# A hybrid convolution-attention kernel on one core: where four branch weights and sixteen filter scales are computed

## The chip, the cores and the metric

The kernel runs on one core of a Trainium2 chip. The metric is the device time of one execution in microseconds. All arithmetic is float32.

## The reference, cut to what matters

The input is `x` of shape (2, 128, 64, 64). Layer 0 normalises it by groups and runs a 7 x 7 neighbourhood attention with its projections and layer norms, then a small feed-forward part. Layer 1 turns the image into 2 x 4096 tokens of 128 channels, adds a self-attention whose queries, keys and values are the same normalised tokens (the diagonal is masked), and then the ffn: a sum over four branches of spectral filters and short lags.

```python
for i, frac in enumerate((1, 2, 4, 8)):
    xi = x[:, :T // frac]
    si = _stu(xi, sigma, phi, M_u[i], M_phi_plus[i], M_phi_minus[i])
    outs.append(jnp.pad(si, ((0, 0), (0, T - si.shape[1]), (0, 0))))
y_soft = softmax((log_weights + gumbel) / TEMPERATURE)
y_hard = one_hot(argmax(y_soft), 4)
weights = y_hard - stop_gradient(y_soft) + y_soft
return jnp.sum(jnp.stack(outs, axis=-1) * weights, axis=-1)
# inside _stu: s = sigma ** 0.25 scales the 16 filters' matrices
```

The weights depend only on `log_weights` and `gumbel`, four numbers each, and the scales only on `sigma`, sixteen numbers.

## The kernel before, in words

The 128 channels or 128 tokens lie on the partitions. **Layer 0** goes through 16 bands (8 per image) of 8 image rows. Each band is cut into named pieces (`p.*` the projections, `u0.*` to `u3.*` the four units of attention, `r.*` and `t.*` what follows it, `k.*` the first tokens of layer 1), and a table `PLAN` gives each piece a due time; a band starts every `PERIOD` = 2300 of the plan's units, so several bands are in flight. All pieces become `events`, sorted by due time, and those in the list `now` are issued inside `tc.manual_schedule` for TensorE (PE), VectorE (DVE), ScalarE (ACT) and GpSimd (POOL): the order on those four queues is the order of the list. SP, which issues the loads and stores (the band's values to memory at L479, its windows back at L496), is not in that set. What is left over of the last bands goes into the list `later`.

**Layer 1** begins with `attention(0, fill)`. It runs over 36 pairs of 512-token chunks; `weights` makes a tile of scores (L905), masks the diagonal (L911, VectorE) and takes the exponential (L913, ScalarE); `turned` transposes tiles (L929) and takes them out with VectorE (L932); L943 and L970 multiply by the tokens. After every other step `fill()` takes one step from the generators in `steps`: first `drain()`, which issues `later` by threes, then `chosen` (the function `branch_weights`), then `filters()`, then `tokens(1, bank)`. `branch_weights` loads `log_w`, `gumbel` and `sigma`, computes `sg = sigma ** 0.25` on GpSimd, the softmax and the one-hot masks in some 23 tiny VectorE instructions, the weights `wt`, the masks `seg` by segment, and at last `mixed(mu, m_u)`, the weighted sum of the branches' short-lag matrices. `attention(1, fill)` does the second image; its steps include `for_ffn`, which opens tiles in the space of the first image's tokens and mixes the ffn's matrices in `filter_matrices` (L1146, L1148, then scaled by `sg` at L1163 and L1164). Then comes the ffn itself, L1379 and L1391, some 900 us of matmuls.

Outside `tc.manual_schedule` the order of each engine's queue is drawn by the compiler from a priority in program order and from what is ready.

Of the kernel before, what the change touches and what calls it, by code (L numbers as in the profile page):

```python
# [8 lines left out]
F32 = mybir.dt.float32  # L9
# [5 lines left out]
P = 128  # L15
# [6 lines left out]
KF = 16  # L22
# [73 lines left out]
def kernel(  # L96
# [62 lines left out]
    mhalf = const.tile([P, KF], F32, name="mhalf")  # L159
    nc.vector.memset(mhalf, -0.5)  # L160
    seg = const.tile([P, NBR], F32, name="seg")


    def rsqrt(dst, var, eps):
# [61 lines left out]
    with l0a:  # L226
# [523 lines left out]
        def behind():  # L750
# [22 lines left out]
            nc.vector.tensor_copy(wg[:, W_2:W_3], pb[:, 0:P])  # L773
            yield

        events = []
        for k, (b, g) in enumerate(order):
            t = {}
# [23 lines left out]
        gn1 = group_norm(1)  # L802
        for i in range(7):
            events.append((2 * PERIOD + i * PERIOD // 3 + 50, None, "", lambda: next(gn1)))
        events.sort(key=lambda e: e[0])


# [52 lines left out]
    with ap_:  # L860
# [11 lines left out]
        tr = tp.tile([P, 2, NC], F32, name="tr")  # L872
        nc.sync.dma_start(out=tr, in_=nc.inline_tensor(t_in, "t_in").ap().rearrange("(h p) c -> p h c", p=P))
        sg = tp.tile([P, KF], F32, name="sg")
        wt = tp.tile([P, NBR], F32, name="wt")
        one = tp.tile([P, 512], F32, name="one")
        nc.gpsimd.memset(one, 1.0)

# [212 lines left out]
                        )  # L1091
                    yield

        def branch_weights():

            lw = sp.tile([P, NBR], F32, tag="lw", name="lw")
            gu = sp.tile([P, NBR], F32, tag="gu", name="gu")
            nc.sync.dma_start(out=lw, in_=log_w.partition_broadcast(P))
            nc.sync.dma_start(out=gu, in_=gumbel.partition_broadcast(P))
            nc.sync.dma_start(out=sg, in_=sigma.partition_broadcast(P))  # L1100
            yield
            quarter = sp.tile([P, KF], F32, tag="quarter", name="quarter")
            nc.gpsimd.memset(quarter, 0.25)
            nc.gpsimd.tensor_tensor(sg, sg, quarter, ALU.pow)

            z = sp.tile([P, NBR], F32, tag="z", name="z")
            nc.vector.tensor_tensor(z, lw, gu, ALU.add)
            m = sp.tile([P, 1], F32, tag="zm", name="zm")
            nc.vector.tensor_reduce(m, z, AX.X, ALU.max)
            nc.vector.tensor_scalar(z, z, m, None, ALU.subtract)  # L1110
            ys = sp.tile([P, NBR], F32, tag="ys", name="ys")
            tot = sp.tile([P, 1], F32, tag="tot", name="tot")
            nc.scalar.activation(ys, z, AF.Exp, bias=0.0, scale=1.0, accum_out=tot)
            nc.vector.reciprocal(tot, tot)
            nc.vector.tensor_scalar(ys, ys, tot, None, ALU.mult)
            yield
            nc.vector.tensor_reduce(m, ys, AX.X, ALU.max)

            oh = sp.tile([P, NBR], F32, tag="oh", name="oh")
            nc.vector.tensor_scalar(oh, ys, m, None, ALU.is_equal)  # L1120
            seen = sp.tile([P, NBR], F32, tag="seen", name="seen")
            nc.vector.tensor_copy(seen[:, 0:1], oh[:, 0:1])
            for i in range(1, NBR):
                nc.vector.tensor_tensor(seen[:, i : i + 1], seen[:, i - 1 : i], oh[:, i : i + 1], ALU.max)
            for i in range(NBR - 1, 0, -1):
                nc.vector.tensor_tensor(oh[:, i : i + 1], seen[:, i : i + 1], seen[:, i - 1 : i], ALU.subtract)
            yield

            for j in range(NBR):
                nc.vector.tensor_copy(seg[:, j : j + 1], seen[:, NBR - 1 - j : NBR - j])  # L1130
            nc.vector.tensor_tensor(wt, oh, ys, ALU.subtract)
            nc.vector.tensor_tensor(wt, wt, ys, ALU.add)

            yield
            mixed(mu, m_u)
            yield

        def mixed(dst, src):
            dst2 = dst.rearrange("p k e -> p (k e)")
            for i in range(NBR):  # L1140
                st = sp.tile([P, 4, P], F32, tag="st", name="st")
                n = src.shape[1]
                nc.sync.dma_start(out=st[:, 0:n], in_=src[i].rearrange("k d e -> d k e"))
                st2 = st[:, 0:n].rearrange("p k e -> p (k e)")
                if i == 0:
                    nc.vector.tensor_scalar(dst2, st2, wt[:, 0:1], None, ALU.mult)  # L1146
                else:
                    nc.vector.scalar_tensor_tensor(dst2, st2, wt[:, i : i + 1], dst2, ALU.mult, ALU.add)  # L1148
# [18 lines left out]
        def filters():  # L1167

            fr = sp.tile([P, 2, 4 * BINS], F32, tag="fr", name="fr", bufs=1)
            nc.sync.dma_start(out=fr, in_=nc.inline_tensor(t_filter, "t_filter").ap().rearrange("(a p) c -> p a c", p=P))  # L1170

            def lags(c0):

                pn = sp.tile([P, KF, 2, LG], F32, tag="st", name="pn")
                nc.sync.dma_start(
                    out=pn.rearrange("p k l f -> p (k l) f"),
                    in_=bass.AP(phi_pad.tensor, P - FB + c0 * FB, [[FB, P], [PHW, 2 * KF], [1, LG]]),
                )
# [12 lines left out]

            def more(m, j):
                banks[m] = bank()
                rows_ = slice(j % 2 * SB, (j % 2 + 1) * SB)
                nc.tensor.matmul(
                    banks[m], lhsT=fr[rows_, j // 2, m * P : (m + 1) * P],
                    rhs=ph[j // 2][rows_].rearrange("p l f k -> p (l f k)"), start=True, stop=True,
                )

            def keep(m, j):  # L1200
                if j == 0:
                    sums[m] = sp.tile([P, 512], F32, tag="sum", name="sum", bufs=2)
                    nc.scalar.copy(sums[m], banks[m])
                else:
                    nc.vector.tensor_tensor(sums[m], banks[m], sums[m], ALU.add)
                nb = P // 4
                nc.sync.dma_start(
                    out=gs[m * nb : (m + 1) * nb, :, SG - 1 - j].rearrange("g r (o c) -> (g r) o c", o=2), in_=sums[m]
                )

            begin = [4 * (m // 2) + m % 2 for m in range(4 * BINS // P)]
            for slot in range(begin[-1] + SG):
                mine = [(m, slot - s0) for m, s0 in enumerate(begin) if 0 <= slot - s0 < SG]
                for mj in mine:
                    more(*mj)
                for mj in mine:
                    keep(*mj)
                yield
# [35 lines left out]
        def drain():  # L1254

            rings[:] = [(ps_m, "bank")] * 2
            for i, f in enumerate(later):
                f()
                if i % 3 == 2:
                    yield  # L1260
            l0.close()
            tp1 = ap_.enter_context(tc.tile_pool(name="l1_t1", bufs=1, side="right"))
            tt[1] = tp1.tile([P, NT, P], F32, name="tt1")
            tok[1] = tp1.tile([P, NT, P], F32, name="tok1")
            cm[1] = tp1.tile([P, T], F32, name="cm1")
            yield

        chosen = branch_weights()
        next(chosen)
        steps = [drain(), chosen, filters(), tokens(1, bank)]  # L1270
        fill, left = filler(0, steps)
        attention(0, fill)
        for gen in steps:
# [28 lines left out]
        def for_ffn():  # L1302

            nonlocal mpl, mmi, inv, mu1, ctp
            while spare != [None]:
                yield True
            first_.close()
            l1 = ctx.enter_context(tc.tile_pool(name="l1", bufs=1))
            mpl = l1.tile([P, KF, P], F32, name="mpl")
            mmi = l1.tile([P, KF, P], F32, name="mmi")  # L1310
            mu1 = l1.tile([P, 3, P], F32, name="mu1")
            inv = l1.tile([P, 3, CB], F32, name="inv")
            ctp = ctx.enter_context(tc.tile_pool(name="blocks", bufs=5))
            nc.gpsimd.tensor_copy(mu1, mu)
            yield from filter_matrices(mpl, mmi)

            nc.sync.dma_start(out=inv, in_=nc.inline_tensor(t_out, "t_out").ap().rearrange("(a p) c -> p a c", p=P))
            for s, (lo, hi) in enumerate(((0, 32), (32, 64), (64, 128), (128, 256))):
                nc.vector.tensor_scalar(inv[:, :, lo:hi], inv[:, :, lo:hi], seg[:, s : s + 1], None, ALU.mult)
            yield  # L1320
            yield from load_blocks()
# [251 lines left out]
```

## Time and profile before

| what | us |
|---|---|
| median of 3 runs | 2194.35 |
| lowest, highest | 2192.41, 2196.59 |
| profiled execution, its own time | 2194.31 |
| its span | 2192.6 |
| TensorE busy | 2141.4 |
| VectorE busy | 952.3 |
| ScalarE busy | 769.8 |
| GpSimd busy | 278.5 |
| L1104, the power of `sg`, GpSimd | 3.17, at 351.48 |
| L1107 to L1132, weights and masks, VectorE | from 342.10 to 348.35 |
| L1143 and on, the ffn's matrices mixed | 945 to 1020 |

The span is the time from the first to the last instruction; the execution's own time has 1.7 us around it. Layer 0 ends at about 340 to 345, the first attention at about 800, the second at about 1290. Durations in the trace are those of single instructions on the engine; those of TensorE are modelled at their ends. Two consecutive instructions of one engine can overlap by a few hundredths of a microsecond.

### The profile page before, as it was taken

What the parts mean: (1) busy time and instruction counts of PE and PEld (TensorE: products, weight loads), DVE (VectorE), ACT (ScalarE), POOL (GpSimd) and SP (SyncE); (2) the same over time, 40 slices, a digit from 0 to 9 for tenths busy, and PEclk for the clock granted to TensorE, in tenths of its full rate; (3) what the DMA queues carried; (4) which work ended last, traced back from release to release, by engine and by line L of the source; (5) the groups of instructions that cost most, each with busy time, mean ns of one, the idle gap of its engine ahead of it and who ended that gap; (6) DMA issues with size and microseconds to landing.
All of it is one profiled execution on the core that took longest, in us unless ns stands there. A gap on an engine that the chain in (4) does not pass through costs nothing.

```text
span 2192.6 us, 32071 instructions
## 1 busy us (share of the span) xinstructions
PE 2141.4 (98%) x12016; PEld 1339.1 (61%) x12016; DVE 952.3 (43%) x3150; ACT 769.8 (35%) x1904; POOL 278.5 (13%) x359
## 2 busy tenths in 40 slices
PE   6899998999999999999999999999999999999998
PEld 4677765545555444544555456776767676767776
DVE  5899986444443353366333543222232323232232
ACT  3889883222332222222223233222232323232232
POOL 3477874200000000000000000000000000000000
PEclk8999999999999999999999999999999999999999
DMA  4222212011000011043000142121221212212101
GB/s 147 62 62 61 62 53 53 0 68 53 25 24 25 19 34 44 1 138 87 1 24 25 49 112 55 45 60 43 57 54 46 52 48 46 54 46 55 40 11 77
DMA packets 170347, 110.56 MB, mean 50 GB/s; under 512 B 21311, under 2 KB 155087, under 8 KB 169680
## 3 DMA queue, kind: packets, MB, share of 16 engines
q1 hardware_dynamic: 169266, 105.01, 17.7%
q8 instruction: 95, 1.56, 0.3%
q0 software_dynamic: 576, 2.10, 0.3%
q10 hardware_dynamic: 350, 1.41, 0.3%
q14 instruction: 60, 0.49, 0.1%
HBM read 73.86 MB, written 34.63 MB: 49 GB/s over the span
## 4 chain that ended last, share of the span: by engine, by line
PE 87%; DVE 5%; POOL 3%; DMA 2%; ACT 1%; issue 1%; SPq 0%; POOLq 0%; DVEq 0%; ACTq 0%
PE acc L1391 26%; PE pc L1379 13%; PE own L943 10%; PE bank L905 9%; PE other L970 8%; PE bank L929 4%; PE bank L335 2%; PE bank L1082 2%; PE bank L545 2%; PE bank L195 2%; PE bank L1034 1%; PE py L1413 1%; DMA st<-in_m_minus_dram 1%; PE bank L509 1%; PE po L567 1%
## 5 line engine op out<-in xcount | busy, mean ns | idle before, releaser
L1380 DVE COPY y<-pc 128x512 f32<-128x512 f32 x320 | 221.3, 692 | 350.8 <-PE pc L1379 347.2
L913 ACT ACTIVATE e<-bank 128x512 f32<-128x512 f32 (+3 forms) x288 | 161.6, 561 | 511.6 <-PE bank L905 384.7
L1391 PE MATMUL acc<-y,mpl 128*128 128x256 f32 x1280 | 292.2, 382 | 0.0
L1391 PE MATMUL acc<-y,mmi 128*128 128x256 f32 x1280 | 288.1, 379 | 0.0
L1379 PE MATMUL pc<-ct,ut 64*128 64x512 f32 x1280 | 285.5, 596 | 0.0
L905 PE MATMUL bank<-cm 128*128 128x512 f32 (+3 forms) x576 | 277.6, 564 | 1.4 <-DVE y L656 1.4
L1391 PEld LDWEIGHTS acc<-y,mpl 128*128 128x128 f32 x1280 | 238.3, 190 | 59.2 <-issue 29.6
L1391 PEld LDWEIGHTS acc<-y,mmi 128*128 128x128 f32 x1280 | 242.8, 190 | 32.4
L1380 ACT COPY y<-pc 128x512 f32<-128x512 f32 x320 | 204.8, 640 | 91.8 <-PE pc L1379 91.7
L943 PE MATMUL own<-et,tok 128*128 128x512 f32 x448 | 227.8, 595 | 4.4 <-DVE part L932 4.3
L970 PE MATMUL other<-e,tok 128*128 128x512 f32 x448 | 229.0, 593 | 0.0
L1379 PEld LDWEIGHTS pc<-ct,ut 64*128 64x128 f32 x1280 | 120.6, 187 | 145.9 <-issue 140.2
L932 DVE CUSTOM_DVE_ANT_0 et<-bank,one 128x512 f32<-128x512 f32 x224 | 145.9, 686 | 121.5 <-PE bank L929 121.2
L1398 ACT COPY ob<-acc 128x256 f32<-128x256 f32 x32 | 19.3, 604 | 387.1 <-PE acc L1391 387.1
L943 PEld LDWEIGHTS own<-et,tok 128*128 128x128 f32 x448 | 83.9, 190 | 113.8 <-issue 65.1
L1415 DVE TENSOR_TENSOR xa<-py,xa 128x512 f32<-128x512 f32 x32 | 22.1, 692 | 281.4 <-PE py L1413 281.4
L970 PEld LDWEIGHTS other<-e,tok 128*128 128x128 f32 x448 | 81.9, 190 | 89.7 <-issue 87.2
L929 PEld LDWEIGHTS bank<-ident,e 128*128 128x128 f32 x896 | 102.9, 141 | 54.3 <-issue 49.3
L905 PEld LDWEIGHTS bank<-cm 128*128 128x128 f32 x576 | 93.9, 191 | 64.1 <-issue 43.5
L167 POOL TENSOR_TENSOR ln_rs<-ln_rs,mhalf 128x4 f32<-128x4 f32 x24 | 24.2, 1007 | 775.4 <-DVE ln_rs L166 775.4
L532 ACT ACTIVATE p<-p,mn 128x196 f32<-128x196 f32 x256 | 114.3, 449 | 14.2 <-DVE mn L522 13.6
L929 PE MATMUL bank<-ident,e 128*128 128x128 f32 x896 | 117.3, 274 | 0.0
(227 smaller groups left out, 2339.8 us busy)
## 6 DMA issues: line engine op xcount, KB each, us to landing
ut<-us SPq DMA_DIRECT2D x80, 256.0 KB
us<-ub SPq DMA_DIRECT2D x64, 256.0 KB
vw<-vd SPq DMA_DIRECT2D x256, 49.0 KB
ct<-gs SPq DMA_DIRECT2D x160, 72.0 KB
ct<-gs SPq DMA_DIRECT2D x160, 64.0 KB
gs<-sum SPq DMA_DIRECT2D x20, 256.0 KB
vd<-v SPq DMA_DIRECT2D x128, 32.0 KB
st<-in_m_plus_dram SPq DMA_DIRECT2D x16, 256.0 KB
```

The costliest lines, as they stand in the source:

```text
L195: nc.tensor.transpose(ps[:, j * P : (j + 1) * P], src[:, j, :], ident)
L335: nc.tensor.matmul(pl, lhsT=wg[:, lo : lo + P], rhs=zT, start=True, stop=True)
L532: nc.scalar.activation(p, p, AF.Exp, bias=t[name + "mn"][:, h : h + 1], scale=-1.0, accum_out=t["den"][:, u, h : h + 1],)
L905: nc.tensor.matmul(ps[:, lo:], lhsT=cm[b][:, n * P : (n + 1) * P], rhs=cm[b][:, CHUNKS[c] * 512 + lo : (CHUNKS[c] + 1) * 512], start=True, ...
L913: nc.scalar.activation(e[:, lo:], ps[:, lo:], AF.Exp, bias=0.0, scale=ASCALE, accum_out=part[:, n, c : c + 1])
L929: nc.tensor.transpose(pt[:, k * P : (k + 1) * P], es[k][:, m * P : (m + 1) * P], ident)
L932: nc.vector.tensor_tensor_reduce(et, pt, one, 1.0, 0.0, ALU.mult, ALU.add, part[:, n, a : a + 1])
L943: nc.tensor.matmul(own, lhsT=tok[b][:, n, :], rhs=e, start=first, stop=last)
L970: nc.tensor.matmul(other, lhsT=tok[b][:, 4 * CHUNKS[a] + j, :], rhs=es[j], start=(j == 0), stop=(j == 3))
L1379: nc.tensor.matmul(pc, lhsT=ut[fp, b, par, :], rhs=cv_[fp], start=True, stop=True)
L1380: (nc.scalar.copy if f else nc.vector.tensor_copy)(y[:, 4 * f : 4 * f + 4, :, par, b * 2 * FB + q : (b + 1) * 2 * FB : 2], pc.rearrange("p ...
L1391: nc.tensor.matmul(acc, lhsT=(mmi if l else mpl)[:, k, :], rhs=y[:, 1::2, k, ::-1, :] if l else y[:, 0::2, k, :, :], start=(l == 0 and k = ...
```

## The change

`branch_weights` moves into layer 0 as four events of the hand-written order, at due times `(len(order) - 4) * PERIOD + 450 * i + 100`, that is in band 12 of 16: its two loads, the softmax, the masks, then `seg` and `wt`. Its tiles move from the layer-1 pool to the `const` pool. `sigma` is no longer loaded there: its load, the memset of 0.25 and the power stand in `for_ffn`, ahead of `filter_matrices`. In layer 1 the four steps of `chosen` become one step, `own_lags`, which holds only `mixed(mu, m_u)`.

```diff
+    wt = const.tile([P, NBR], F32, name="wt")
...
+        def branch_weights():
+            lw = const.tile([P, NBR], F32, name="lw")
+            gu = const.tile([P, NBR], F32, name="gu")
+            nc.sync.dma_start(out=lw, in_=log_w.partition_broadcast(P))
+            nc.sync.dma_start(out=gu, in_=gumbel.partition_broadcast(P))
+            yield
+            z = const.tile([P, NBR], F32, name="lw_gu")
+            nc.vector.tensor_tensor(z, lw, gu, ALU.add)
...
+            nc.scalar.activation(ys, z, AF.Exp, bias=0.0, scale=1.0, accum_out=tot)
+            nc.vector.reciprocal(tot, tot)
+            nc.vector.tensor_scalar(ys, ys, tot, None, ALU.mult)
+            yield
+            nc.vector.tensor_reduce(m, ys, AX.X, ALU.max)
+            oh = const.tile([P, NBR], F32, name="oh")
+            nc.vector.tensor_scalar(oh, ys, m, None, ALU.is_equal)
...
+            yield
+            for j in range(NBR):
+                nc.vector.tensor_copy(seg[:, j : j + 1], seen[:, NBR - 1 - j : NBR - j])
+            nc.vector.tensor_tensor(wt, oh, ys, ALU.subtract)
+            nc.vector.tensor_tensor(wt, wt, ys, ALU.add)
+            yield
...
+        weights_ = branch_weights()
+        for i in range(4):
+            events.append(((len(order) - 4) * PERIOD + 450 * i + 100, None, "", lambda: next(weights_)))
         events.sort(key=lambda e: e[0])
...
-        def branch_weights():
-            lw = sp.tile([P, NBR], F32, tag="lw", name="lw")
...
-            nc.sync.dma_start(out=sg, in_=sigma.partition_broadcast(P))
-            yield
-            quarter = sp.tile([P, KF], F32, tag="quarter", name="quarter")
-            nc.gpsimd.memset(quarter, 0.25)
-            nc.gpsimd.tensor_tensor(sg, sg, quarter, ALU.pow)
...
-            yield
-            mixed(mu, m_u)
-            yield
...
-        chosen = branch_weights()
-        next(chosen)
-        steps = [drain(), chosen, filters(), tokens(1, bank)]
+        def own_lags():
+            mixed(mu, m_u)
+            yield
+
+        steps = [drain(), own_lags(), filters(), tokens(1, bank)]
...
             nc.gpsimd.tensor_copy(mu1, mu)
+            nc.sync.dma_start(out=sg, in_=sigma.partition_broadcast(P))
+            quarter = sp.tile([P, KF], F32, tag="quarter", name="quarter", bufs=1)
+            nc.gpsimd.memset(quarter, 0.25)
+            nc.gpsimd.tensor_tensor(sg, sg, quarter, ALU.pow)
             yield from filter_matrices(mpl, mmi)
```

More of the change, by code (lines that the diff above doesn't have):

```diff
@@ L774, in behind @@
             yield
+        def branch_weights():
[6 more added lines that the diff above has]
+            nc.vector.tensor_tensor(z, lw, gu, ALU.add)
+            m = const.tile([P, 1], F32, name="zm")
+            nc.vector.tensor_reduce(m, z, AX.X, ALU.max)
+            nc.vector.tensor_scalar(z, z, m, None, ALU.subtract)
+            ys = const.tile([P, NBR], F32, name="ys")
+            tot = const.tile([P, 1], F32, name="tot")
+            nc.scalar.activation(ys, z, AF.Exp, bias=0.0, scale=1.0, accum_out=tot)
[5 more added lines that the diff above has]
+            nc.vector.tensor_scalar(oh, ys, m, None, ALU.is_equal)
+            seen = const.tile([P, NBR], F32, name="seen")
+            nc.vector.tensor_copy(seen[:, 0:1], oh[:, 0:1])
+            for i in range(1, NBR):
+                nc.vector.tensor_tensor(seen[:, i : i + 1], seen[:, i - 1 : i], oh[:, i : i + 1], ALU.max)
+            for i in range(NBR - 1, 0, -1):
+                nc.vector.tensor_tensor(oh[:, i : i + 1], seen[:, i : i + 1], seen[:, i - 1 : i], ALU.subtract)
+            yield
[4 more added lines that the diff above has]
+            yield
         events = []
@@ L874 @@
         sg = tp.tile([P, KF], F32, name="sg")
-        wt = tp.tile([P, NBR], F32, name="wt")
         one = tp.tile([P, 512], F32, name="one")
@@ L1092, in short_lags @@
                     yield
-        def branch_weights():
-            lw = sp.tile([P, NBR], F32, tag="lw", name="lw")
-            gu = sp.tile([P, NBR], F32, tag="gu", name="gu")
-            nc.sync.dma_start(out=lw, in_=log_w.partition_broadcast(P))
-            nc.sync.dma_start(out=gu, in_=gumbel.partition_broadcast(P))
-            nc.sync.dma_start(out=sg, in_=sigma.partition_broadcast(P))
-            yield
-            quarter = sp.tile([P, KF], F32, tag="quarter", name="quarter")
-            nc.gpsimd.memset(quarter, 0.25)
[L1104 to L1115, printed above, removed]
-            yield
[L1117 to L1126, printed above, removed]
-            yield
[L1129 to L1134, printed above, removed]
-            mixed(mu, m_u)
-            yield
         def mixed(dst, src):
```

## The prediction

> **What bounds the kernel now.** I read the page's first line of totals, then stretches by engine, then the chain of waits and the timeline around the two places that the edit touches.
>
> ```profile
> PE 2141.4 (98%) x12016; PEld 1339.1 (61%) x12016; DVE 952.3 (43%) x3150; ACT 769.8 (35%) x1904; POOL 278.5 (13%) x359
> ```
>
> TensorE fills 98% of 2192.6 us, so a change that adds no matmul can only win back the 51 us in which it is not busy, or make more of them. The stretches (us; busy time of each engine and, in brackets, instructions; then granted clock, DMA share, GB/s) say where they lie:
>
> ```profile
> 219.00:274.00 55.00, 54.77 (x812) 40.86 (x811) 51.77 (x275) 49.31 (x153) 48.65 (x62) 1.00 0.23 62
> 301.00:320.00 19.00, 17.35 (x273) 12.59 (x272) 15.60 (x84) 14.94 (x48) 13.47 (x18) 1.00 0.22 63
> 320.00:340.00 20.00, 16.94 (x239) 12.03 (x237) 12.45 (x63) 12.09 (x38) 11.51 (x16) 0.83 0.22 64
> 340.00:366.00 26.00, 22.21 (x119) 12.28 (x118) 18.25 (x80) 8.62 (x26) 21.09 (x23) 1.00 0.39 70
> 366.00:900.00 534.00, 529.59 (x1893) 265.96 (x1894) 220.44 (x751) 149.29 (x401) 31.54 (x36) 1.00 0.10 30
> ```
>
> The reader is to see three regimes. In layer 0's steady bands (219 to 274) four engines are close to full: VectorE 94%, ScalarE 90%, GpSimd 88%, and the chain of work passes from one to the next, so there a microsecond on VectorE is not free. From 301 to 366, the end of layer 0 and the start of layer 1, TensorE idles 1.65 + 3.06 + 3.79 = 8.5 us. From 366 to 900 it lacks 4.4 us in 534: nothing placed there shows.
>
> **What the Trainium skill says.** "TensorE: Matmul & The Clock Gate", Part 1, says that the clock falls to half after an idle window of some 3.4 us and that the window runs freely. The trace agrees: the clock is 0.50 from about 332.9 to 339.7, 6.8 us, hence the 0.83 above. "VectorE: DVE Perf Modes", The DRAIN you can't avoid, says that each VectorE instruction pays a flush before the next starts. The trace's 128x4 operations, each fed by the one before, start 0.18 to 0.20 us apart for a few elements. "Perfetto Trace Analysis", Tensor Engine Instruction, says that VectorE, ScalarE and GpSimd run strictly in order; the waits below agree.
>
> **Part 1: the weights leave the start of layer 1.** The timeline today (start, duration, engine, line; in brackets the idle time before it):
>
> ```profile
> 342.10 0.15 DVE L1107 TENSOR_TENSOR z<-lw,gu 128x4 f32<-128x4 f32 x1
> 343.27 0.23 DVE L1115 TENSOR_SCALAR ys<-ys,tot 128x4 f32<-128x4 f32 x1
> 345.78 0.80 DVE L1120 TENSOR_SCALAR oh<-ys,zm 128x4 f32<-128x4 f32 x1
> 347.80 0.29 DVE L911 TENSOR_TENSOR bank<-bank,ndiag 128x128 f32<-128x128 f32 x1
> 348.25 0.60 ACT L913 ACTIVATE e<-bank 128x512 f32<-128x512 f32 x1 [5.21 <-DVE wt L1131]
> 351.48 3.17 POOL L1104 TENSOR_TENSOR sg<-sg,quarter 128x16 f32<-128x16 f32 x1
> 354.22 0.36 DVE L695 BATCH_NORM_AGGREGATE kmv<-ln_st 128x2 f32<-128x6 f32 x4
> 354.67 0.23 POOL L700 TENSOR_SCALAR krs<-kmv 128x4 f32<-128x4 f32 x1
> ```
>
> The first softmax tile of layer 1 waits for L911, and L911 stands behind the masks. VectorE ends `y` at 345.86 and the first matmul of L905 (346.01, four in 1.74 us, so 0.43 each) is done by about 346.5. Without L1120 to L1130 L911 could start at 346.55, that is 1.25 us sooner, and TensorE idles 1.24 us just then (347.75 to 348.99). The `mixed(mu, m_u)` operations stay and become ready sooner, and two of them (0.62 each) may take that place: the gain is 0 to 1.25 us, 1.0 by choice. ScalarE loses 0.39 us of exponential and read-out here, and SP the issue of two small loads (0.36 + 0.41 us); both engines idle around them, so these count nothing.
>
> But GpSimd has a chain of its own, almost gapless from 340.44 to 360.66, and TensorE's next stall (0.81 us before 366.56) comes out of it: L932 stands on VectorE behind a `z` that waits for GpSimd's L389. If the `sg` power keeps its place, GpSimd is free at 354.65 whatever VectorE won, and the gain is given back at 366. Today the power costs nothing either: `kmv` ends at 354.58 and `krs` starts at 354.67.
>
> **Part 2: sigma's load, memset and power are written into `for_ffn`.** Written later is not run later: outside the hand-ordered part, queues take what is ready. Two rows show it, one a load of the ffn's matrices whose reader runs at 945, one a memset of the second attention that ran before the second attention began (its other memset is at 804.72):
>
> ```profile
> 357.14 0.37 SPq L1143 DMA_DIRECT2D st<-in_m_plus_dram  x1
> 716.81 0.10 POOL L1299 MEMSET tt<- 128x2 f32 x1 [20.88 <-PE bank L195]
> ```
>
> So the likeliest place of the power is the hole at 351.5 again, and of part 1's 1.0 us I keep 0.3. If it does run at 945 instead, GpSimd's one `mu` copy is done at 945.51 and its next work comes at 1022.36; 0.11 + 3.17 us end near 949 after the load's issue (0.47 us) and landing, and `sg` is first read at 964.50. That cover is 15 us, so the cost is nothing; the bound is 0 to +0.5 us (operations on VectorE run longer beside GpSimd: 0.80 for L1120 against 0.23 for its like, L1115).
>
> **Part 3: the same work enters layer 0, in a fixed order.** The four pieces are due at 27,700, 28,150, 28,600 and 29,050 of the plan, band 12 of 16. By the plan's neighbours, piece two falls on VectorE between L383/L398 and `t.y` (L656), and on ScalarE between `t1.za` (L409) and a copy:
>
> ```profile
> 281.48 0.36 DVE L383 BATCH_NORM_AGGREGATE ln_mv<-ln_st 128x2 f32<-128x6 f32 x4
> 281.80 1.11 DVE L656 SCALAR_TENSOR_TENSOR y<-bank,ln_rs,add 128x128 f32<-128x128 f32 x4
> 281.36 0.57 ACT L552 COPY pT<-bank 98x512 f32<-98x512 f32 x1
> ```
>
> VectorE's bill: piece two 1.40 us (today 342.10 to 343.50, with 0.36 us of waiting for ScalarE); piece three a reduce 0.19, the compare 0.25, a copy 0.19, three maxima 0.57, three differences 0.24, together 1.44; piece four 4 copies at 0.07, then 0.19 and 0.16, together 0.63. Sum 3.5 us. New waits: ScalarE reaches the exponential near 281.4, VectorE ends the subtraction near 282.4, so ScalarE stands about 1 us with the copy `pT` behind it, for which TensorE's L567 waits; VectorE then stands 0.36 us with `y`, `z` and the L522 masks behind it, for which ScalarE's L532 and TensorE's banks wait. VectorE has no idle time from 274 to 291, so all of it is passed on at first. What gives way is seen in the waits (164 to 301; total, times, longest):
>
> ```profile
> DVE ln_nb L398 <- POOL ln_rs L389: 5.0, 6, 0.9
> ```
>
> About one such wait (0.95 us at 291.3) falls in the shifted stretch and GpSimd, busy with `tok`, doesn't move with VectorE there; with 0.25 us from the waits on TensorE after it I take 1.2 us as recovered. Cost 2.3 us, from 0.5 (the 11 us of VectorE's idle time between 301 and 340 take most of it) to 4.5 (nothing recovered and ScalarE's 1 us on top). The two loads go to tiles that nothing held before. SP is idle from the last start-up load to the first store, so I expect them there, and they are landed long before they are read:
>
> ```profile
> 9.64 0.35 SPq L287 DMA_DIRECT2D tok<-window_masks  x1
> 30.63 9.95 SPq L479 DMA_DIRECT2D vd<-v  x16
> ```
>
> The steps of `filters` and `tokens` come up three fill slots earlier, in the stretch without room: 0, plus or minus 1 us of other order.
>
> **Sum.** +2.3 - 0.3 + 0 = +2.0 us. The profiled execution took 2194.31 us (span 2192.6), the median of the runs is 2194.35, so both stand alike: 2196.3 us. About 0.2%, 4.4 us, is what a measurement of this kernel can tell from no change.
>
> **Rivals.**
> *A, as summed*, the loss in layer 0 and the gain after it within 0.2%: own range 2191.5 to 2198.7, chance 0.60. It includes the case that the change doesn't do what it says for sigma, and the one where it does.
> *B, faster*: layer 0 loses 0.5, part 1 gains 1.25 and the 0.81 us stall at 366 too, and the end of layer 0, shifted, escapes the half clock. TensorE is busy 6.0 of those 6.8 us, so 3.0 us less. 0.5 - 1.25 - 0.8 - 3.0 = -4.6: 2189.7. For it: 8.5 us of idle time sit there. Against: layer 0's gaps that lead to the low clock remain. Chance 0.12.
> *C, slower*: nothing recovered (+4.5) and the half clock lasts a window longer (3.4 us at half rate, +1.7): +6.2, 2200.5. It decides from 4.4 us on. For it: the full engines at 219 to 301. Chance 0.20.
> *D, slower*: the loads of piece one are not issued early but stand in SP's queue in band 12. SP is issuing nearly all the time there (stores from 275.69, then loads 280.75 to 293.72); behind those they would land near 296.8 (0.77 to issue, about 2.3 as the `st` load of 348.91 took until its reader started at 351.24), 14.9 us after VectorE wants them: 2211 with part 3. It decides once the issue comes later than about 279.5. Against: the early issues shown. Chance 0.08.
>
> The range 2190.5 to 2201.5 takes in A and most of C. Faster 0.12, same 0.60, slower 0.28.
>
> **What would show it.** Right: `lw` and `gu` issued before 30; L911 at about 346.5 after its matmul, not behind masks; band 12 longer by 2 to 3.5 us, with ScalarE waiting about 1 us for L1110's successor; the power still between 340 and 400. Wrong: bands 12 to 15 no longer than before (part 3), VectorE waiting for `lw` (D), the clock at half for 3.4 or 10 us (B or C), or TensorE's idle time from 366 to 1300 changed by over 2 us.

## The result, and the profile after

Over the six runs of each kernel, the changed one takes 2204.38 us in the median (2202.02 to 2205.43) and the one before 2194.59 (2192.41 to 2196.59): ratio 1.004, 95% interval 1.003 to 1.005. It is slower by 9.8 us in the medians, and the prediction said 2196.3 with an upper end of 2201.5. The profiled execution took 2205.24 us, its span is 2203.5, against 2194.31 and 2192.6 before. In kernel.py the lines have moved: L905, L911, L913 are now L944, L950, L952; L522 and L532 are L523 and L533; the power L1104 is L1315; the mixing L1146 and L1148 is L1141 and L1143; the copies L1181 are L1176. The weights lie at L781 to L810.

The line of totals of the page, after:

```profile
PE 2147.2 (97%) x12016; PEld 1342.3 (61%) x12016; DVE 952.3 (43%) x3150; ACT 770.4 (35%) x1904; POOL 278.1 (13%) x359
```

No engine has more work: VectorE's 952.3 us is the number of before. TensorE shows 5.8 us more with the same 12016 matmuls; some of that is clock (27.3 us at half rate, 20.5 before, without the stretch at the end of each profile), and the other 5 us of the span are waiting. The first of the stretches shown before (busy time of each engine, then granted clock, DMA share, GB/s):

```profile
219.00:274.00 55.00, 51.95 (x759) 38.54 (x756) 52.11 (x276) 45.82 (x144) 46.85 (x59) 0.98 0.22 62
```

In these full bands TensorE was busy 54.77 of 55 us. It is now busy 2.8 us less, and ScalarE 3.5 us less, while VectorE is as full as it was: VectorE did other work and they waited. The timeline after, around the weights and at the start of layer 1, with rows left out:

```profile
263.00 0.15 DVE L785 TENSOR_TENSOR lw_gu<-lw,gu 128x4 f32<-128x4 f32 x1
268.21 0.39 DVE L798 TENSOR_SCALAR oh<-ys,zm 128x4 f32<-128x4 f32 x1
268.82 1.50 DVE L802 TENSOR_TENSOR seen<-seen,oh 128x1 f32<-128x1 f32 x3
...
352.69 0.48 DVE L950 TENSOR_TENSOR bank<-bank,ndiag 128x128 f32<-128x128 f32 x2
353.05 0.60 ACT L952 ACTIVATE e<-bank 128x512 f32<-128x512 f32 x1 [5.48 <-DVE bank L950]
356.17 2.93 POOL L1315 TENSOR_TENSOR sg<-sg,quarter 128x16 f32<-128x16 f32 x1
360.80 0.36 DVE L696 BATCH_NORM_AGGREGATE kmv<-ln_st 128x2 f32<-128x6 f32 x4
361.25 0.23 POOL L701 TENSOR_SCALAR krs<-kmv 128x4 f32<-128x4 f32 x1 [2.16 <-DVE kmv L696]
```

Three things are new. The weights run at 263 to 273, not at 282. ScalarE's first exponential of layer 1 waited 5.21 us before and waits 5.48 now, although the masks are gone. And GpSimd's `krs` now waits 2.16 us for `kmv`; before, it followed the power at once. (`kmv` is VectorE's mean and variance of the last tokens of layer 1, `krs` the scale that GpSimd makes of it; the normalised tokens `tok` wait for both.)

**Where the time went.** I paired every instruction of VectorE, ScalarE and GpSimd in two profiles by its source text, its tiles and its ordinal number, and took, at each instruction, the median of the 25 differences of start from there on. The table gives how much this delay against the first profile of the kernel before grew in each stretch (us; times are those of the kernel before). The first column of numbers holds the bands with the weights, the third the first stage of layer 1, the fifth attention 0, the last the mixing of the ffn's matrices. The 1.21 from 360 to 372 are a window of half clock at 367 or 369. In the stretch from 300 to 345 the first profile of the kernel before has two windows of half clock (332.9 to 339.7), so a minus there says mostly that another execution had fewer.

| profile | 235 to 300 | 300 to 345 | 345 to 360 | 360 to 372 | 420 to 692 | 940 to 1030 |
|---|---|---|---|---|---|---|
| after | +4.43 | -0.13 | +1.42 | +1.21 | +0.94 | +2.82 |
| after, second profile | +3.31 | -1.34 | +1.41 | 0.00 | +0.91 | +3.21 |
| before, second profile | -0.02 | +0.22 | +0.07 | -0.01 | +0.01 | +0.91 |
| sigma alone | -0.01 | -0.97 | +0.05 | 0.00 | +0.02 | +2.37 |
| weights alone | +4.32 | -1.56 | +2.17 | 0.00 | +0.94 | +2.38 |
| no weights | -0.02 | +0.05 | +1.04 | 0.00 | +1.22 | +2.52 |
| steps padded | +4.45 | -0.11 | +1.56 | +1.21 | +0.03 | +1.96 |
| weights in the early hole | -0.03 | -2.48 | +1.21 | 0.00 | +1.03 | +3.78 |
| phi behind kmv | +3.28 | -1.31 | +0.55 | 0.00 | +0.91 | +2.25 |
| three remedies | -0.02 | -0.89 | +0.23 | 0.00 | +0.02 | +3.35 |
| three remedies, aligned | -0.02 | +0.21 | +0.24 | 0.00 | +0.01 | +2.10 |

Four stretches carry the loss, and each has its own experiment below. The delay is just changing at 345, so the two columns that meet there can trade some 0.5 us. Taken together, from 341 to 364, both profiles of the changed kernel lose 0.9 us net: 0.7 are gained by 350, since the masks are gone, 2.2 are lost at `krs`, and 0.6 won back.

### The profile page after: what moved, and what is told of

It is laid out like the page before. It is cut to its first block, busy times and chain, and to the rows that moved or that the text cites. A ratio compares the mean times of both kernels' runs of the same rounds, so it can differ in the third digit from the quotient of the medians.

```text
span 2203.5 us, 32071 instructions
## 1 busy us (share of the span) xinstructions
PE 2147.2 (97%) x12016; PEld 1342.3 (61%) x12016; DVE 952.3 (43%) x3150; ACT 770.4 (35%) x1904; POOL 278.1 (13%) x359
## 3 DMA queue, kind: packets, MB, share of 16 engines
q8 instruction: 95, 1.56, 0.3%
q10 hardware_dynamic: 350, 1.41, 0.2%
## 4 chain that ended last, share of the span: by engine, by line
PE 86%; DVE 5%; DMA 3%; POOL 3%; ACT 1%; SPq 1%; issue 1%; DVEq 0%; ACTq 0%; POOLq 0%
PE acc L1392 25%; PE pc L1380 13%; PE own L982 10%; PE bank L944 9%; PE other L1009 8%; PE bank L968 4%; PE bank L336 2%; PE bank L1121 2%; PE bank L196 1%; PE bank L1073 1%; PE bank L546 1%; PE py L1414 1%; DMA st<-in_m_minus_dram 1%; PE bank L510 1%; PE po L568 1%; DMA st<-in_m_plus_dram 1%
## 5 line engine op out<-in xcount | busy, mean ns | idle before, releaser
L952 ACT ACTIVATE e<-bank 128x512 f32<-128x512 f32 (+3 forms) x288 | 161.6, 561 | 515.8 <-PE bank L944 388.3
L944 PE MATMUL bank<-cm 128*128 128x512 f32 (+3 forms) x576 | 278.7, 566 | 1.4 <-DVE y L657 1.4
L944 PEld LDWEIGHTS bank<-cm 128*128 128x128 f32 x576 | 94.4, 192 | 64.5 <-issue 43.8
L533 ACT ACTIVATE p<-p,mn 128x196 f32<-128x196 f32 x256 | 114.4, 449 | 16.1 <-DVE mn L523 15.3
```

What stands on the lines that cost most here:

```text
L533: nc.scalar.activation(p, p, AF.Exp, bias=t[name + "mn"][:, h : h + 1], scale=-1.0, accum_out=t["den"][:, u, h : h + 1],)
L944: nc.tensor.matmul(ps[:, lo:], lhsT=cm[b][:, n * P : (n + 1) * P], rhs=cm[b][:, CHUNKS[c] * 512 + lo : (CHUNKS[c] + 1) * 512], start=True, ...
L952: nc.scalar.activation(e[:, lo:], ps[:, lo:], AF.Exp, bias=0.0, scale=ASCALE, accum_out=part[:, n, c : c + 1])
```

## The experiments

My theory after the first profile of each kernel: the layer-0 bands lose about 5 us, the earlier fill slots of the filters lose 1.5 to 2.5 at `krs` and in attention 0, and the mixing of the matrices loses up to 3 for a reason not yet known. Rivals: the half-clock stretches decide and only move about; sigma's later load delays the mixing.

### The two parts apart

`sigma_only` is the kernel before with this edit, `weights_only` the changed kernel with it reversed:

```diff
-            nc.sync.dma_start(out=sg, in_=sigma.partition_broadcast(P))   # in branch_weights
-            quarter = ...; nc.gpsimd.memset(quarter, 0.25)
-            nc.gpsimd.tensor_tensor(sg, sg, quarter, ALU.pow)
+            # the same lines in for_ffn, ahead of filter_matrices
```

> The kernel before with one part of the change: sigma's load, the constant quarter and the power go to the place where the ffn's matrices are mixed; weights and masks stay at the start of layer 1. The part is innocent by itself: the power is scheduled into a hole of GpSimd ahead of krs in either place and the filters keep their slots, so theory one (the cost lies in layer 0 and in the filters' earlier slots) expects 2194.5 within 2, ratio 0.999 to 1.001. Theory two (the later load or the power delays the mixing of the matrices, where after lost 2.8 us) expects 2197 to 2198, and m_plus and m_minus waits of VectorE 2 us above the kernel before.

Measured: 2195.90 us against 2195.37, ratio 1.0005 (0.9999 to 1.0012). The power runs at 350.02 for 3.27 us, ahead of `krs`, as in the kernel before. Sigma's part is innocent up to 945 us; its +2.37 in the mixing stretch came as theory two had it, but see `weights_only`.

> The changed kernel with sigma's load, quarter and power put back at the start of layer 1; weights and masks stay in layer 0, and the filters stand two fill slots earlier than in the kernel before. Theory one (layer 0 costs 5, the filters' order 1.5 to 2.5, the mixing stretch 0 to 3): 2201 to 2204.5, ratio 1.003 to 1.005 on the kernel before. If the two parts were to blame together (the power moved behind, the copies of phi moved ahead of kmv), 2199 to 2200.

Measured: 2204.66 us, ratio 1.0044 (1.0032 to 1.0057). The whole loss is in the weights' part. And its mixing stretch is 2.38 us late too, with sigma's load at its old place: so sigma's lateness is not what slows the mixing.

### The bands of layer 0

`no_weights` drops the weights' four events and fills `seg` and `wt` with constants:

```diff
-        weights_ = branch_weights()
-        for i in range(4):
-            events.append(((len(order) - 4) * PERIOD + 450 * i + 100, None, "", lambda: next(weights_)))
+    nc.gpsimd.memset(wt, 0.25); nc.gpsimd.memset(seg, 0.25)
```

> The changed kernel without the computation of the branches' weights and masks: both are filled with 0.25 at the start, so this part of the computation is left out. The rest of the change stays (filters three slots earlier, sigma at the ffn's matrices). Theory one: the work in band 12 of layer 0 is worth 5 us as it stands: 2198.5 to 2200.5, and the start of layer 1 comes at the time of the kernel before. Rival: the clock's half-rate stretch decides and moves with everything; then 2202 to 2206 or 2195 to 2196, whichever stretch it falls in.

Measured: 2199.07 us, ratio 1.002 (1.0012 to 1.0029), about 5.3 us under the changed kernel. The delay in the bands is -0.02: it is all the weights' doing. The 3.7 us that stay above the kernel before belong to the later stretches.

`masks_twice` does the masks' step twice:

```diff
+            for _ in range(2):
                 nc.vector.tensor_reduce(m, ys, AX.X, ALU.max)
...
```

> The changed kernel with the masks' step in band 12 done twice over, the second time into the same tiles: 2.5 us more on VectorE there, nothing else. If VectorE's time in this band is paid in full: 2.5 more between 255 and 300 us, 2206.5 to 2207.2. If a third is won back, as the prediction had it: 1.6 more, 2206. If the cost is in the handshakes of the single insertions (ScalarE's exponential, the late mean): under 1 more.

Measured: 2206.73 us, ratio 1.0049 (1.0035 to 1.0063). The two passes in its timeline:

```profile
268.64 1.50 DVE L805 TENSOR_TENSOR seen<-seen,oh 128x1 f32<-128x1 f32 x3
...
271.02 0.55 DVE L805 TENSOR_TENSOR seen<-seen,oh 128x1 f32<-128x1 f32 x3
```

My 2.5 us was wrong: the second pass runs from 270.39 to 271.97, 1.58 us, since its three maxima take 0.55 in place of 1.50. The bands' delay grows from 4.43 to 6.07 us, by 1.64: what is put on top is paid in full. The size alone (1.6) would have suited the other reading, that a third of 2.5 is won back; the timeline decides.

Why the same three maxima took 1.50 us and then 0.55 can be read off GpSimd's timeline. First GpSimd in the changed kernel, then the same maxima in `early_aligned` (below), where no GpSimd operation ran beside them:

```profile
268.66 1.41 POOL L641 TENSOR_TENSOR x<-x,xa 128x128 f32<-128x128 f32 x2
```

```profile
26.84 0.55 DVE L803 TENSOR_TENSOR seen<-seen,oh 128x1 f32<-128x1 f32 x3
```

GpSimd's two operations end at 269.12 and 270.07. Of VectorE's maxima, the first runs from 268.82 to 269.13 and the second from 269.17 to 270.08: they end with GpSimd's operations, and alone they take 0.16 us each. The compare ahead of them, 0.39 us, ends at 268.60, and GpSimd's L639 at 268.58. All eight profiles with the weights in band 12 show these pairs of ends. In the second pass GpSimd ran L707, a TENSOR_SCALAR, and the maxima took 0.16 us each beside it. (One case doesn't fit: in the kernel before the first maximum took 0.43 us beside L638, a TENSOR_SCALAR, and no GpSimd operation ended with it.) So the masks cost more than their size because of what GpSimd ran at that moment.

`early_weights` puts the same instructions where VectorE was idle. In the changed kernel it waited 6.28 us for the first `kT` matmuls, from 26.5 to 32.8:

```profile
32.80 0.87 DVE L464 TENSOR_SCALAR kT<-bank,cb 128x128 f32<-128x128 f32 x2 [6.28 <-PE bank L336]
```

One more step boundary, behind the exponential, isn't shown in the cut.

```diff
-        for i in range(4):
-            events.append(((len(order) - 4) * PERIOD + 450 * i + 100, ...
+        for at in (FIRST.index("w"), FIRST.index("f2") + 0.5, *[FIRST.index("p.kT0") - 0.5] * 3):
+            events.append((at - 1000, None, "", lambda: next(weights_)))
```

> The changed kernel with the four weight steps taken out of band 12 and put at the very start of layer 0: sums and exponential after the second flip of the masks, the rest ahead of the first kT eviction, where VectorE stood idle for 6.28 us. Theory one (layer 0 costs what VectorE's time costs in a full band, and nothing in a hole): the delay of 4.4 us between 255 and 300 us goes, 2199 to 2200.5. Rival (the chain of small dependent instructions costs wherever it stands, through ScalarE or the late kT): 2203 to 2205.

Its timeline:

```profile
24.59 0.16 DVE L785 TENSOR_TENSOR lw_gu<-lw,gu 128x4 f32<-128x4 f32 x1 [2.38 <-DMA gu<-in_gumbel_dram]
28.75 1.09 DVE L803 TENSOR_TENSOR seen<-seen,oh 128x1 f32<-128x1 f32 x3
31.95 0.87 DVE L464 TENSOR_SCALAR kT<-bank,cb 128x128 f32<-128x128 f32 x2 [0.85 <-PE bank L336]
```

The whole computation fits, and `kT` still waits 0.85 us for TensorE; the delay in the bands is -0.03, and ahead of the table's first column nothing is lost either: the delay is 0.0 at 10 us and -1.1 at 35, behind the hole. The median, though, is 2202.73 us, ratio 1.0026 (1.0014 to 1.0037): 2 us above what I expected. The profiled execution, 2198.83, is the fastest of the six, and it has 13.7 us at half clock where the first profile of the kernel before has 20.5. The other five were granted a lower mean clock, 0.992 to 0.994 against 0.996, and so ran longer at half rate; where, no trace shows. So this run shows the place to be free and not the whole gain; the combined kernels below carry the gain.

### The start of layer 1 and the fill slots

`padded_steps` gives the filters their old slots:

```diff
         def own_lags():
+            for _ in range(3):
+                yield
             mixed(mu, m_u)
```

> The changed kernel with three empty fill slots ahead of the mixing of mu, so that the filters and tokens come in the slots that they have in the kernel before. Theory one: the two copies of phi stand behind kmv again, krs comes 1.5 to 2 us earlier, and the drift in attention 0 goes as well: 2201.5 to 2203 against 2204.4, of which the 5 us of layer 0 stay. Rival: the slots are indifferent and the later start is only carried by the half-clock stretch; then 2204.4 within 1.

Measured: 2203.01 us, ratio 1.0038 (1.0026 to 1.0051). Half of the theory fell. The delay of attention 0 goes from 0.94 to 0.03, so the earlier slots cost 0.9 us there. But the copies of phi (the filters' input, loaded as `pn`) stood ahead of `kmv` as in the changed kernel, and 1.56 us stay at `krs`: it isn't the slot that brought them forward. In the kernel before they come behind `kmv`, which starts at 354.22:

```profile
356.28 0.83 DVE L1181 COPY ph<-pn 128x256 f32<-128x256 f32 x2 [0.66 <-DMA pn<-in_phi_pad_dram]
```

With the weights gone, the sums of `mu` stand earlier in VectorE's queue, ahead of the last `y` (347.29, `y` at 349.75) and not behind it. They and phi's loads use the same buffers `st`. My reading is that these come free earlier by the compiler's reckoning, so that phi's loads and copies go in there; no run shows that reckoning. The changed kernel's timeline shows what the new order does on the chip:

```profile
356.89 0.68 DVE L1176 COPY ph<-pn 128x256 f32<-128x256 f32 x2 [1.43 <-DMA pn<-in_phi_pad_dram]
359.43 0.68 DVE L1176 COPY ph<-pn 128x256 f32<-128x256 f32 x2 [1.38 <-DMA pn<-in_phi_pad_dram]
```

VectorE stands 2.81 us for two loads, with `kmv` behind them. `pn_own` gave the loads other buffers:

```diff
-                pn = sp.tile([P, KF, 2, LG], F32, tag="st", name="pn")
+                pn = sp.tile([P, KF, 2, LG], F32, tag="ub", name="pn", bufs=3)
```

> The changed kernel with phi's loads in the buffers of the tag ub, which are free at the start of layer 1, so that they don't queue behind mu's pieces in st and the copies no longer wait ahead of kmv. Theory one (the copies' waits of 1.43 and 1.38 us made kmv and krs late): krs 1.5 to 2 us earlier against the start of layer 1, 2202.4 to 2203. Rival (the power on GpSimd ends no earlier than kmv and decides): 2204.4 within 0.7.

A miss: 2206.90 us, ratio 1.0047 (1.0035 to 1.006), and a net loss of 4.2 us from 341 to 364, where the changed kernel has 0.9. The copies were now put even further ahead, in front of `mu` and of work that TensorE needs:

```profile
349.55 0.87 DVE L1176 COPY ph<-pn 128x256 f32<-128x256 f32 x1 [1.77 <-DMA pn<-in_phi_pad_dram]
...
353.77 2.71 PE L944 MATMUL bank<-cm 128*128 128x512 f32 x4 [3.54 <-DVE y L657]
```

The first line is VectorE waiting 1.77 us at the head of the queue, the second TensorE waiting 3.54 us for the `y` behind it. `early_all` held the same edit with the two others:

> The changed kernel with three edits together: weight steps in VectorE's hole at the start of layer 0, phi's loads in buffers of their own, three empty fill slots ahead of mu's mixing. If the three delays (4.4 in layer 0, 1.5 to 2 at krs, 0.95 by the slots of the filters) are separate and add: 2197 to 2198, and within 1 us of the kernel before up to 940 us. If the half-clock stretches take it back: 2199 to 2201.

2202.29 us, ratio 1.0026 (1.0015 to 1.0037), with a net loss of 4.5 in the same place: missed for the same reason. `phi_after` moves no load and ties the copies down instead:

```diff
+                nc.vector.tensor_copy(ph[:, :, 0, 0], tt[0][:, NT - 4, 0:2])
                 for l in range(2):
                     nc.vector.tensor_copy(ph[:, l], pn[:, :, l, ::-1].rearrange("p k f -> p f k"))
```

> The changed kernel with the copies of phi tied behind kmv: a copy of two elements per partition from the last tokens into the copies' target makes them wait for what kmv waits for. No load moves. Theory (the copies, waiting for pn on DMA ahead of kmv, delay krs by 1.4 to 2 us): the delay between 345 and 360 falls to 0 to 0.5, and 2202.5 to 2203.2 against 2204.4. Rival (TensorE or GpSimd's power set that time): the delay stays at 1.4 or more and 2204.4 within 0.7.

GpSimd's `krs` in its timeline:

```profile
357.40 0.23 POOL L701 TENSOR_SCALAR krs<-kmv 128x4 f32<-128x4 f32 x1 [0.30 <-DVE kmv L696]
```

It waits 0.30 us in place of 2.16, and the stage loses 0.55 instead of 1.41 in the table's column, 0.0 instead of 0.9 net from 341 to 364. The median is 2202.21 us, ratio 1.0032 (1.002 to 1.0045), beside 2203.96, ratio 1.0039 (1.0026 to 1.0051), of the changed kernel beside it: the medians alone would not tell the two apart. Second profiles of the two kernels:

> The kernel before, unchanged, for a second profile. In the stretch from 945 to 1020 us, where the ffn's matrices are mixed, every other kernel so far took 2.0 to 3.8 us longer than the first profile of the kernel before. If the change's sigma or its tiles cause that, this profile agrees with the first one within 0.5 us there. If it is the DMAs of one execution, this one also stands 1.5 to 3.5 us above the first. The stretches of half clock should stand elsewhere, or be another number, if they are of the execution.

> The changed kernel, unchanged, for a second profile and for its median beside the two kernels below. 2204 within 1.5. What belongs to the program must come again: 4.4 us between 255 and 300, 1.5 to 2.1 between 345 and 360, 0.95 between 420 and 690. What belongs to the execution moves: the half-clock stretches at 271, 319 and 367 us, and the mixing stretch by up to 1 us.

The one of before took 2195.91 us. What belongs to the program came again (1.41 and 0.91 us), and the half clock at 319 and 367 did not. The bands lost 3.31 us, not 4.43; the matmul that VectorE had kept waiting tells why, first in the first profile, then in the second:

```profile
270.99 1.81 PE L336 MATMUL bank<-zT,w_sb 128*128 128x512 f32 x2 [1.99 <-DVE mn L523]
```

```profile
270.90 1.13 PE L336 MATMUL bank<-zT,w_sb 128*128 128x512 f32 x2 [1.99 <-DVE mn L523]
```

The wait is the same; in the first a window of half clock (271.3 to 274.7) follows, which makes two matmuls 1.81 us in place of 1.13 and adds 1.1 us in all. Such a window at this place appears in five of the eight profiles with the weights in band 12, and in none of the eleven without them. That the stall brings it on is likely by this count, and not shown by an experiment.

`early_order` puts the three remedies together: the early hole, phi behind `kmv`, the padded slots.

> The changed kernel with all three remedies: weight steps in VectorE's hole at the start of layer 0, copies of phi behind kmv, three empty fill slots ahead of mu's mixing. Against the kernel before: 0 in layer 0, 0 to 0.5 at krs, 0 in attention 0. If these were the change's whole cost: 2195.5 to 2197.5, no different from the kernel before by more than 0.1 per cent. If a cost is left that I haven't named: 2199 or more.

2198.17 us, ratio 1.0013 (1.0007 to 1.002): not equal to the kernel before. Its rows in the table are near zero but for the last: the mixing stretch, +3.35.

### The mixing of the ffn's matrices

On VectorE and SP the order there is that of the kernel before, but for one swapped pair on VectorE, and VectorE waits for the pieces `st`. What every kernel but the one before had changed is where tiles lie: the change takes tiles from a pool of layer 1 and adds nine to `const`, and `st` goes from byte 137984 of a partition, a multiple of 256, to 137952. Four kernels change the place alone. The first three append 8, 16 and 64 unused numbers to sigma's tile in the kernel before:

```diff
-        sg = tp.tile([P, KF], F32, name="sg")
+        sg = tp.tile([P, KF + 8], F32, name="sg")[:, 0:KF]
```

> The kernel before with eight unused numbers per partition appended to sigma's tile: no instruction and no order changes, but the small pool with st, ub and sum lies 32 bytes lower, at the address that it has in the changed kernel (137952, no multiple of 64, in place of 137984, a multiple of 256). If the place of the DMAs' targets makes the mixing of the ffn's matrices slower: the stretch from 945 to 1020 us takes 2 to 3 us more than in the kernel before, and 2197 to 2198 against 2195.2. If not: within 1 us in that stretch, 2195.2 within 1.

> The kernel before with 16 unused numbers per partition after sigma's tile: no instruction and no order changes, st, ub and sum lie 64 bytes lower (st at 137920, a multiple of 64 and not of 256, its place in the kernel with sigma's part alone). If a place off the multiples of 256 bytes costs: 2 to 3 us more than the first profile of the kernel before from 945 to 1020 us, and about 1.3 us in the median. If only a place off the multiples of 64 costs: within 1 us in the stretch.

> The kernel before with 64 unused numbers per partition after sigma's tile: everything in the small pool lies 256 bytes lower, st again at a multiple of 256 (137728). If it is the alignment: within 1 us of the kernel before in the stretch from 945 to 1020 us, and the same median within 0.7. If any move costs, or if the first profile of the kernel before was merely a lucky one: 2 us or more in the stretch.

VectorE's waits from 945 to 1024 us (total, times, longest), first 256 bytes lower, then 32 bytes lower:

```profile
DVE mmi L1148 <- DMA st<-in_m_minus_dram: 9.3, 8, 3.1
DVE mpl L1148 <- DMA st<-in_m_plus_dram: 6.0, 8, 1.6
```

```profile
DVE mmi L1148 <- DMA st<-in_m_minus_dram: 11.2, 9, 4.0
DVE mpl L1148 <- DMA st<-in_m_plus_dram: 7.3, 8, 1.6
```

Against the first profile of the kernel before, the stretch lost 3.72 us at 32 bytes, 2.83 at 64 and 0.94 at 256, which is what the second profile of the kernel before lost (0.91). The medians follow, each within its noise: 2197.47 us, ratio 1.0007 (0.9998 to 1.0015); 2197.15, 1.0006 (0.9998 to 1.0015); 2195.10, 1.0001 (0.9993 to 1.0009). In the other direction, unused room in three small tiles of the changed kernel brings `st`, `ub`, `ct`, `mpl` and `inv` back to their old remainders of 512 bytes:

```diff
-            lw = const.tile([P, NBR], F32, name="lw")
+            lw = const.tile([P, NBR + 56], F32, name="lw")[:, 0:NBR]
...
-            quarter = sp.tile([P, KF], F32, tag="quarter", name="quarter", bufs=1)
+            quarter = sp.tile([P, KF], F32, tag="quarter", name="quarter", bufs=8)
```

> The changed kernel with unused room in three small tiles, so that st, ub, ct, mpl and inv lie at the same remainder of 512 bytes as in the kernel before; no instruction and no order changes. If the addresses cost the 2.8 us of the mixing stretch: 2201 to 2202 against 2204.2, and that stretch within 1 us of the kernel before. If not: 2204.2 within 1.

2202.03 us, ratio 1.0025 (1.0015 to 1.0034). The stretch lost 1.52 us in place of 2.82 and 3.21, and at the start of layer 1 the stage lost 0.49 in place of 1.4: phi's loads go to `st` as well, and VectorE waited 0.35 us for the first of them, not 1.43. From 341 to 364 nothing is lost net (0.0), although the copies still stand ahead of `kmv`. So the loss at `krs` took both the copies' new place in the queue and the lateness of their loads; each remedy alone removes it.

> The three remedies together (weight steps in VectorE's hole, phi's copies behind kmv, the filters' slots) and the addresses of the kernel before. If the four causes are all: 2195.2 within 1, no difference from the kernel before. If the addresses are nothing: 2198.2 as with the three remedies alone.

2196.53 us against 2196.20 of the kernel before, ratio 0.9998 (0.999 to 1.0007): no difference within about 2 us either way, as expected if the four causes are all; its own profile still loses 2.10 us in the mixing. Over all profiles the stretch loses 1.1 us on the mean of the five with `st` at a multiple of 256 (0 to 2.10), and 2.9 on the mean of the fourteen without (1.96 to 3.78): 1.8 us. That the place costs is shown by the kernels that change nothing else, with one profile each, and in the profiles rather than in the medians. The Trainium skill, "DMA: Bandwidth & Descriptors", How a descriptor splits into AXI transactions, says that when a descriptor doesn't start at a multiple of 256 bytes, its first piece begins at the boundary below, and the bytes ahead of the start are fetched unused and still cost time. That speaks of what is fetched, and here it is the loads' target that moved. The direction agrees; that this is the cause here no run shows.

## Why the prediction was wrong, point by point

The steps that failed are the term of the masks in part 3, which was sized too small, and three things that the sum put at nothing or did not have: the copies of phi, the fill slots and the tiles' place.

**Part 3, the bill.** VectorE's bill was 3.5 us; it is 4.4: 1.31 for the softmax (1.40 predicted), 0.66 for `seg` and `wt` (0.63), and some 2.4 for the masks, where the sum had 1.44. The mis-sized parts are the three maxima, 0.57 by the durations of their like, 1.50 on the chip, and the compare, 0.25 against 0.39, both run beside GpSimd as shown at `masks_twice`. I had the warning in hand: the 0.80 us of L1120 in the timeline of before I put down to GpSimd, and used it only as a bound on part 2, although GpSimd is 88% busy in the bands to which part 3 moves this work.

**Part 3, what is recovered.** I took 1.2 us as won back, and this was right in kind and nearly in size. The wait that gave way is of the kind named, one band earlier; in the kernel before it is

```profile
273.28 0.16 DVE L398 SCALAR_TENSOR_TENSOR ln_nb<-ln_mv,ln_rs 128x4 f32<-128x4 f32 x1 [0.94 <-POOL ln_rs L389]
```

In the second profile of the changed kernel this wait is gone, and the delay falls there from 4.3 to 3.3 us. I had the place of band 12 wrong by one band (281 instead of 263). ScalarE's wait for the exponential was right: 0.98 us, about 1 predicted. The larger wait, to which I gave no size, came after the masks in VectorE's queue, where TensorE stood 1.99 us for L523.

**The clock.** Rival C had the half clock lengthened by a window at the end of layer 0, +1.7 us. What came is a window inside band 12, behind that stall, for 1.1 us. The skill's section on the clock, cited in the prediction, holds for the length: all stretches of half clock in these profiles, but the one at the end of each, are 3.4, 6.8, 10.2 or 13.7 us long, whole multiples of one window. Its idle window does not fit, and the prediction's "the trace agrees" was too quick: TensorE was busy 1.4 of the 3.4 us ahead of 271.3, and 2.5 of the 3.4 us ahead of 332.9 in the kernel before. In the second profile of the changed kernel the same stall had no window behind it.

**Part 1.** Right up to `krs`: the masks' leaving won 0.7 us by 350 (0 to 1.25 predicted), ScalarE's first exponential came 0.2 us sooner against layer 0's delay, and `mu`'s sums took the place ahead of L950, as the text allowed. That most of the gain is given back at GpSimd shows in `phi_after`, where all of it is (0.3 kept by the prediction). But the step stopped there. It said that GpSimd's power decides `krs`; it did not ask what the compiler would move into the time that the weights leave free on VectorE. The copies of phi went in, on loads that came late, and 0.3 us of gain became 0.9 us of loss.

**Part 2.** Right: the power ran at 356.17, in the hole ahead of `krs`, and sigma's part by itself costs nothing up to 945 us.

**The fill slots.** "0, plus or minus 1 us": the sign was left open and it was 0.9 us in attention 0, shown by `padded_steps`.

**The addresses.** The prediction has no such step. It looked at where the loads of `lw` and `gu` would stand (right: SP issued them at 9.25 and 18.27 us, so rival D was wrong), and not at what else the tiles' move would shift.

So 3.3 + 0.9 + 0.9 + 1.8 = 6.9 us by the program, and 1.1 more where the window of half clock comes: 6.9 to 8.0 us, where the runs show 1.0039 of 2195, 8.6 us, with an interval from 5.7 to 11.2, and 9.8 us in the first six. The terms are those of single profiles but for the 1.8, a mean over all kernels; the two profiles of each of the two kernels alone would give 2.6 in its place. What the sum lacks may be clock: the granted clock is 0.9934 on the mean of the changed kernel's eleven runs and 0.9947 in the runs of the kernel before beside the experiments. By these figures I estimate some 6 us more at half rate, of which at most half is lost, and 1.1 of that is counted. No run shows which of these windows the change brings on. The prediction had 2.0.

## What to carry to other kernels

Work that was moved into an engine's full stretch cost its time here, less what a later wait absorbed (4.3 less 1.0 us); in a hole of that same engine it cost nothing (the 6.28 us up to 32.8), and a timeline shows such holes directly. Price tiny operations of VectorE by what GpSimd runs beside them in the new place, not by their durations in the old one. When work leaves a place that a compiler orders, ask what it will put there and whether that new tenant waits for a load. And compare the addresses of DMA targets before and after an edit that only adds or removes small tiles.

## What I had not expected of the hardware

The place of a load's target in SBUF showed: the same loads with `st` 32 or 64 bytes off its place made the mixing stretch 3.7 and 2.8 us longer in 75, and 256 bytes off no longer than a second profile of the unchanged kernel (0.9 both). Tiny operations of VectorE ended only with GpSimd's operation beside them: three 128x1 maxima took 1.50 us beside a TENSOR_TENSOR of GpSimd and 0.55 beside a TENSOR_SCALAR or alone. Two profiles of one program differed by 1.1 us in one stretch through a single window of half clock, which followed 3.4 us in which TensorE was busy for 1.4.
